# Storing the second layer's edge coefficients in the first pass over the edges of a graph kernel

## The chip, the core and the metric

The kernel runs on one core of a Trainium2 chip. The metric is the device time of one execution in microseconds (us). Three executions of the kernel before gave 28895.52, 28902.54 and 28908.87 us; the median is 28902.54 us. A separate execution was recorded by the hardware profiler; it took 34449.25 us, and its span from the first to the last instruction is 34447.5 us. The two figures are kept apart throughout: durations come from the profiled execution, the comparison of kernels from the others.

The engines are TensorE (PE; its weight loads stand as PEld), VectorE (DVE), ScalarE (ACT), GpSimd (POOL) and SyncE (SP). SP, ACT and POOL also issue DMA transfers. SBUF is the memory of the engines, PSUM the one into which PE writes.

## The reference

There are N = 30000 nodes with 128 features each and E = 960000 edges, sorted by destination. Two residual graph layers follow one another; each begins with a layer norm and a ReLU of the node features. The first is made of two relational convolutions with the same edges:

```python
W   = einsum('rb,bdf->rdf', coeff, basis)     # 32 relations from 8 bases
Hr  = einsum('nd,rdf->nrf', h, W)
msg = Hr[src, etype] * norm                   # norm: one weight for each edge
agg = segment_sum(msg, dst, num_segments=N) + bias
```

The first convolution uses `basis1` and `coeff1` and ends in a ReLU, the second `basis2` and `coeff2`. The second layer is gated: with four edge types t, it sums sigmoid(k[dst] + q[src]) * v[src] over the edges of each type and averages the types.

For an edge of relation r with weight w, the kernel needs only the 8 numbers w * coeff[r, 0..7]. These are the edge's coefficients. The relation and the weight are the same in both convolutions; the coefficient table is not.

## The kernel before, in words

**Three passes over the edges.** After a preparation (layer norm, tables of edge offsets) the kernel makes three passes, called c1, c2 and g: the two convolutions, then the gate. An edge tile is 128 edges; three tiles are a group, five groups a block, twenty blocks (100 groups, 300 tiles) an iteration, and each pass is a hardware loop of 25 iterations with the twenty blocks written out (lines 312 to 327). So a pass has 7500 tiles and 500 blocks.

**One tile of c1 or c2.** GpSimd fetches the 128 source rows of 512 bytes with an indirect DMA into `hg` (line 435). VectorE builds `sb`, 128 edges by 8 bases by 32 destinations, in one instruction: where the edge's offset `relc` equals the column number held in `iw`, it puts the edge's coefficient `ce`, elsewhere zero (line 439). TensorE multiplies the two and sums the three tiles of a group in the PSUM tile `pa` (line 445). ScalarE copies `pa` to `ab` (line 449). Once per block TensorE multiplies `ab` by the eight bases into `po` (line 407, 8 multiplications, each of which stands as two records in the profile[...]). VectorE adds `po` to the running sums `agg` of all nodes, window by window, two blocks later (line 359).

**The coefficients of a block** (lines 376 to 402). SyncE loads the relations of the block's edges as `er`, each repeated on 32 partitions, 256 KB (`types`, line 378). VectorE compares them with the partition number into the one-hot `oh` (`onehot`, line 385). TensorE multiplies four 128-column parts of `oh` by the coefficient table (line 390; 32 columns: 4 edge quarters by 8 bases) into `pc`, which is a part of the PSUM tile `cp`. VectorE multiplies `pc` by the edge weights `nrm` into `ce` (`coefficients`, line 399). Both passes do all of this.

**The order of the work.** It is written out by hand; each engine works through its queue in that order. In block s, `types(s + 2)` is issued at the start; `bases_out(s - 1)` follows group 1, `coefficients(s + 1)` group 2, `onehot(s + 2)` and the additions of block s - 2 group 3. At the start of an iteration stand `loads(0)`, `types(0)`, `onehot(0)`, `coefficients(0)`, `types(1)`, `onehot(1)`, ahead of the first `sb` (lines 412 to 417); at its end stand the last `bases_out` and the additions of the last two blocks (lines 461 to 463). `cp` also holds `iw`, which every `sb` reads.

**Buffers.** `hg` has five buffers of one group each: the gathers of group n + 5 wait until TensorE has used group n. `sb` has twelve buffers of one tile, `pa` three, `er`, `oh` and `ce` two. Beside the edges, each pass carries node work in its queues (line 460, `beside`): `after_first` in c1, `after_second` in c2, every ninth group.

Of the kernel before, what the change touches and what calls it, by code (L numbers as in the profile page):

```python
# [9 lines left out]
F32 = mybir.dt.float32  # L10
# [8 lines left out]
P = 128  # L19
# [7 lines left out]
R = 32  # L27
B = 8
T = 4
TP = 128  # L30
NT = E // TP
G = 3
# [37 lines left out]
def kernel(  # L70
# [39 lines left out]
    kcode = nc.dram_tensor("kcode", (E,), F32, kind="Internal").ap()  # L110
    qidx = nc.dram_tensor("qidx", (TP, NT), I32, kind="Internal").ap()

    def gather(to, table, idx):
# [28 lines left out]

    basis, coeff = [], []
    for i, (bas, cof) in enumerate(((basis1, coeff1), (basis2, coeff2))):
        ct = consts.tile([P, 4, B], F32, name=f"coeff{i}")
        nc.vector.memset(ct, 0.0)
        for q in range(4):
            nc.scalar.dma_start(ct[q * R:(q + 1) * R, q, :], cof)
        basis.append(bas)
        coeff.append(ct)  # L150

# [142 lines left out]
    def sorted_path():  # L294
        with ExitStack() as all_:
            def edge_pass(name, body, after, banks, extra=None):


                with ExitStack() as held:
                    weights = held.enter_context(tc.tile_pool(name=f"{name}_w", bufs=1))  # L300
                    steps, run = after(weights), body(weights)
                    with tc.tile_pool(name=f"{name}_io", bufs=NQ) as io, \
                            tc.tile_pool(name=f"{name}", bufs=2) as pool, \
                            tc.tile_pool(name=f"{name}_n", bufs=1) as npool, \
                            tc.tile_pool(name=f"{name}_nps", bufs=banks, space=PSUM) as nps, \
                            tc.tile_pool(name=f"{name}_c", bufs=1, space=PSUM) as cps, \
                            tc.tile_pool(name=f"{name}_ps", bufs=2, space=PSUM) as ps:
                        cp = cps.tile([P, 4 * D], F32, name="cp")
                        iw, ic = cp[:, :W], cp[:, W:W + 1]
                        nc.vector.tensor_copy(iw, irow)  # L310
                        nc.vector.tensor_copy(ic, icol)
                        with tc.For_i(0, NI, 1, iteration_sync="staggered") as i:
                            with tc.manual_schedule():
                                todo = {}
                                for n, step_ in extra(i, npool) if extra else ():
                                    todo.setdefault(n, []).append(step_)
                                for u in range(NPI // VB):
                                    at = i * -NPI + (N + LAG + u * VB)
                                    for n, step in steps(at, npool, nps):
                                        todo.setdefault(u * PERIOD + n, []).append(step)  # L320
                                assert W < TQ * 4 * B and max(todo) < NG

                                def beside(n):
                                    for step in todo.get(n, ()):
                                        step()

                                run(i, io, pool, ps, cp, iw, ic, beside)
# [32 lines left out]

            def rel_body(table, weights, cof):
                def start(npool):
# [4 lines left out]
                def body(bas, i, io, pool, ps, cp, iw, ic, beside):  # L367
                    stage = {}
                    er, oh, pc, ce, ab, po, base = {}, {}, {}, {}, {}, {}, {}

                    def loads(k):
                        stage[k] = [stage_tile(io, "idx", src, I32, i, k),
                                    stage_tile(io, "relc", reld, F32, i, k),
                                    stage_tile(io, "nrm", norm, F32, i, k, 4 * TQ - S * G)]

# [7 lines left out]
                    def onehot(s):  # L383
                        oh[s] = pool.tile([P, TQ, TP], F32, name="oh")
                        nc.vector.tensor_scalar(oh[s], er[s], icol4, None, op0=ALU.is_equal)
                        at = (1 + s % 2) * TQ * 4 * B
                        pc[s] = cp[:TP, at:at + TQ * 4 * B].rearrange("p (c q b) -> p c q b",
                                                                      c=TQ, q=4)
                        for c in range(TQ):
                            nc.tensor.matmul(pc[s][:, c].rearrange("p q b -> p (q b)"),  # L390
                                             lhsT=oh[s][:, c, :],
                                             rhs=cof.rearrange("p q b -> p (q b)"),
                                             start=True, stop=True)

                    def coefficients(s):
                        ce[s] = pool.tile([TP, 4, TQ, B], F32, name="ce")
                        t0 = s % SB * S * G
                        nrm = stage[s // SB][2][:, t0:t0 + 4 * TQ]
                        nc.vector.tensor_mul(
                            ce[s], pc[s].rearrange("p c q b -> p q c b"),  # L400
                            nrm.rearrange("p (q c) -> p q c", q=4).unsqueeze(3).to_broadcast(
                                [TP, 4, TQ, B]))

# [8 lines left out]
                    loads(0)  # L412
                    types(0)
                    onehot(0)
                    coefficients(0)
                    types(1)
                    onehot(1)
                    for s in range(NS):
# [6 lines left out]
                        if s % SB == 2:  # L425
                            leave_stage()
                        idx, relc, _ = stage[k]
                        if s + 2 < NS:
                            types(s + 2)
                        ab[s] = pool.tile([P, B, S, W], F32, name="ab")  # L430
                        for g in range(S):
# [5 lines left out]
                            for j in range(G):  # L437
# [3 lines left out]
                                    relc[:, t0 + j:t0 + j + 1],  # L441
                                    ce[s].rearrange("p q c b -> p (q c) b")[
                                        :, g * G + j, :].unsqueeze(2).to_broadcast([TP, B, W]),
                                    op0=ALU.is_equal, op1=ALU.mult)
# [5 lines left out]
                            if g == 1 and s:  # L450
                                bases_out(s - 1)
                            if g == 2 and s + 1 < NS:
                                coefficients(s + 1)
                            if g == 3 and s + 2 < NS:
                                onehot(s + 2)
                            if g == 3 and s > 1:
# [269 lines left out]

            edge_pass("c1", rel_body(h0, basis[0], coeff[0]), after_first, 2, codes)
            edge_pass("c2", rel_body(h1, basis[1], coeff[1]), after_second, 2)
            edge_pass("g", lambda weights: gate_body, after_third, 1)


    def any_path():
        with ExitStack() as all_:
# [60 lines left out]
            def rel_conv(table, to, weights, cof, relu):  # L794
                bas = cs.tile([P, B, D], F32, name="bas", bufs=2)
                nc.scalar.dma_start(bas, weights.rearrange("b d f -> d b f"))
                with tc.tile_pool(name="slow", bufs=2) as pool, \
# [18 lines left out]
                    for j in range(G):  # L816
                        nc.tensor.matmul(pc[:, j, :], lhsT=oh[:, j, :], rhs=cof[:R, 0], start=True,
                                         stop=True)
# [23 lines left out]

            rel_conv(h0, agg1, basis[0], coeff[0], False)
            rel_conv(agg1, agg2, basis[1], coeff[1], True)

# [116 lines left out]
```

## Time and profile before

| | before |
|---|---|
| median of three executions | 28902.54 us |
| profiled execution | 34449.25 us |
| its span | 34447.5 us |
| POOL busy in the span | 21410.1 us (62%) |
| PE busy | 20497.2 us (60%) |
| DVE busy | 12592.8 us (37%) |
| ACT busy | 3659.3 us (11%) |
| first to last gather of c1 | 192.6 to 11386.4 us |
| of c2 | 11431.9 to 22747.1 us |
| of g | 22865.2 to 34419.0 us |

A line of a group of instructions names the source line, the engine, the operation and the tiles (written first, then read), the number of instructions, the busy time and the mean of one, and then the idle time of the engine just before them with what ended most of it. "issue" means that nothing which the profile shows was waited for. "remote" stands where a semaphore was raised at a moment that fits the end of no recorded instruction. In a timeline the two figures ahead of the engine are the start and the length in us, and the bracket gives the idle time before and what ended it; several instructions of a kind in a row share one line.

### The profile page before, as it was taken

Reading aid. Unit: us, or ns where it says so; the run is one execution under the profiler, and the core shown is the slowest. Engines: PE = TensorE matmul, PEld = TensorE weight load, DVE = VectorE, ACT = ScalarE, POOL = GpSimd, SP = SyncE. Lnnn points to the kernel's source line nnn. Section 1 sums busy time; section 2 is a strip of 40 time slices with the busy share of each in tenths; the row PEclk is TensorE's granted clock in tenths of the full one; section 3 lists DMA queues with packets and bytes.
Section 4 is the critical chain, followed back from the end, with each engine's and each line's share of the span. In section 5 each row is a group of like instructions: output and inputs, shape, how many; then the busy total and the mean of one; then the engine's idle time right before and its main releaser. Section 6 shows DMA issues by size and latency. Waiting matters only on the chain. (4 is left out here: it accounts for less than half of the span.)

```text
span 34447.5 us, 320361 instructions
## 1 busy us (share of the span) xinstructions
PE 20497.2 (60%) x87408; PEld 17662.1 (51%) x87408; DVE 12592.8 (37%) x33274; ACT 3659.3 (11%) x9905; POOL 21410.1 (62%) x22514
## 2 busy tenths in 40 slices
PE   4555555555555566666666666665555555555555
PEld 3444544444444445545555454445555555555555
DVE  3333333333333333333333333333333333333333
ACT  1000000000000111111111111111111111111111
POOL 5666666666666566666666666656666666666666
PEclk7777777777777777777777777765555555555555
DMA  3222222222222222222222222234444444444444
GB/s 97 62 62 62 63 61 62 63 63 62 62 62 62 70 73 73 73 74 72 72 73 73 73 73 73 73 107 145 145 144 144 144 144 146 145 144 144 146 143 141
DMA packets 2182999, 3244.35 MB, mean 94 GB/s; under 512 B 551918, under 2 KB 1559594, under 8 KB 2181290
## 3 DMA queue, kind: packets, MB, share of 16 engines
q0 software_dynamic: 840000, 1967.52, 20.6%
q1 hardware_dynamic: 993620, 1001.65, 9.0%
q10 hardware_dynamic: 347670, 254.20, 2.6%
q8 instruction: 852, 13.96, 0.2%
q14 instruction: 857, 7.02, 0.1%
HBM read 2969.29 MB, written 252.28 MB: 94 GB/s over the span
## 5 line engine op out<-in xcount | busy, mean ns | idle before, releaser
L114 POOL DMA_INDIRECT hg<-h,idx x15000 | 14273.0, 952 | 8446.5 <-issue 4105.1
L445 PE MATMUL pa<-sb,hg 128*128 128x256 f32 x30000 | 9304.2, 468 | 5934.2 <-issue 2892.9
L445 PEld LDWEIGHTS pa<-sb,hg 128*128 128x128 f32 x30000 | 6919.2, 240 | 7715.2 <-issue 3346.1
L114 POOL DMA_INDIRECT qv<-qvtab,qi x7500 | 7109.3, 948 | 4562.6 <-issue 2220.3
L439 DVE SCALAR_TENSOR_TENSOR sb<-cp,relc,ce 128x256 f32<-128x256 f32 x15000 | 6134.1, 476 | 6576.0 <-remote 4679.9
L510 PE MATMUL po<-sel,msg 128*128 128x32 f32 x15000 | 3471.0, 388 | 4592.1 <-DVE msg L508 3824.5
L510 PEld LDWEIGHTS po<-sel,msg 128*128 128x128 f32 x15000 | 3420.4, 328 | 4894.5 <-DVE msg L508 3986.6
L499 PE MATMUL pk<-kw,kb 128*128 128x128 f32 x15000 | 3973.5, 438 | 219.5 <-DVE kb L486 178.4
L540 DVE TENSOR_TENSOR pk<-pk,qv 128x384 f32<-128x384 f32 x2500 | 1406.8, 563 | 7074.9 <-remote 4837.9
L449 ACT COPY ab<-pa 128x256 f32<-128x256 f32 x5000 | 1816.6, 373 | 20148.8 <-remote 8809.6
L499 PEld LDWEIGHTS pk<-kw,kb 128*128 128x128 f32 x15000 | 3466.7, 331 | 222.3 <-issue 222.3
L407 PE MATMUL po<-ab,bas 128*128 128x160 f32 x16000 | 2431.3, 306 | 311.2 <-ACT ab L449 262.8
L407 PEld LDWEIGHTS po<-ab,bas 128*128 128x128 f32 x16000 | 2356.8, 196 | 408.4 <-ACT ab L449 291.0
L359 DVE TENSOR_TENSOR agg<-agg,po 128x32 f32 x7500 | 1402.9, 187 | 2742.5 <-remote 709.7
L541 ACT ACTIVATE pk<-pk 128x384 f32<-128x384 f32 x2500 | 1186.7, 475 | 9493.7 <-DVE pk L540 6531.3
L390 PE MATMUL cp<-coeff,oh 128*128 128x32 f32 x8000 | 1313.4, 297 | 1472.0 <-issue 1173.2
L390 PEld LDWEIGHTS cp<-coeff,oh 128*128 128x128 f32 x8000 | 1394.2, 237 | 1530.9 <-issue 1308.1
L637 PE MATMUL bank<-wall,hT 128*120 128x512 f32 x1572 | 1012.0, 765 | 710.2 <-issue 307.3
L508 DVE TENSOR_TENSOR msg<-pk,qv 128x384 f32<-128x384 f32 x2500 | 1368.0, 548 | 19.4 <-remote 19.4
L486 DVE TENSOR_TENSOR kb<-kb,cp 128x1920 f32<-128x1920 f32 x500 | 1072.7, 2145 | 52.0 <-issue 29.6
L637 PEld LDWEIGHTS bank<-wall,hT 128*120 128x120 f32 x1572 | 345.9, 235 | 988.0 <-issue 581.2
L648 DVE TENSOR_TENSOR kt<-bank,ball 120x512 f32<-120x512 f32 x262 | 181.2, 692 | 1484.0 <-remote 509.2
(77 smaller groups left out, 3762.9 us busy)
## 6 DMA issues: line engine op xcount, KB each, us to landing
kb<-kcode SPq DMA_DIRECT2D x500, 960.0 KB
er<-in_et_row SPq DMA_DIRECT2D x1000, 256.0 KB
hg<-h,idx POOLq DMA_INDIRECT x15000
kw<-ktab SPq DMA_DIRECT2D x2500, 64.0 KB
qvtab<-qvt ACTq DMA_DIRECT2D x262, 480.0 KB
qv<-qvtab,qi POOLq DMA_INDIRECT x7500
ktab<-kt ACTq DMA_DIRECT2D x262, 240.0 KB
xt<-in_x SPq DMA_DIRECT2D x262, 60.0 KB
```

Of the source, the lines that this page charges most:

```text
L114: nc.gpsimd.indirect_dma_start(out=to, out_offset=None, in_=table, in_offset=bass.IndirectOffsetOnAxis(ap=idx, axis=0))
L359: nc.vector.tensor_add(to, to, po[:, g, :])
L390: nc.tensor.matmul(pc[s][:, c].rearrange("p q b -> p (q b)"), lhsT=oh[s][:, c, :], rhs=cof.rearrange("p q b -> p (q b)"), start=True, stop ...
L407: nc.tensor.matmul(po[s].rearrange("p s w -> p (s w)"), lhsT=bas[:, b, :], rhs=ab[s][:, b].rearrange("p s w -> p (s w)"), start=(b == 0), ...
L439: nc.vector.scalar_tensor_tensor(sb, iw[:TP].unsqueeze(1).to_broadcast([TP, B, W]), relc[:, t0 + j:t0 + j + 1], ce[s].rearrange("p q c b - ...
L445: nc.tensor.matmul(pa.rearrange("p b w -> p (b w)"), lhsT=hg[:, j, :], rhs=sb.rearrange("p b w -> p (b w)"), start=(j == 0), stop=(j == G ...
L449: nc.scalar.copy(ab[s][:, :, g, :], pa)
L499: nc.tensor.matmul(pk[n][:, j, :], lhsT=kb[n // S][:, n % S, j * TP:(j + 1) * TP], rhs=kw[n], start=True, stop=True)
L508: nc.vector.tensor_mul(msg, pk[n], qv[n][:, :, 1, :])
L510: nc.tensor.matmul(po[s][:, g, :], lhsT=msg[:, j, :], rhs=sel[s][:, g * G + j, :], start=(j == 0), stop=(j == G - 1))
L540: nc.vector.tensor_add(pk[n], pk[n], qv[n][:, :, 0, :])
L637: nc.tensor.matmul(bank(a, VB, T * D), lhsT=hT, rhs=wall[:, a].rearrange("p t f -> p (t f)"), start=True, stop=True)
```

## The change

The first pass forms the coefficients of both convolutions, since edges and weights are the same. The coefficient table becomes one tile with both layers side by side, so that a one-hot multiplication gives 64 columns instead of 32. Two multiplications by the edge weights follow, one for each layer. The second layer's result is stored by ScalarE's queue into a new DRAM tensor `ce2`, 128 rows of 480 bytes for each block. The second pass has no `er`, no `nrm`, no `onehot` and no `coefficients`; SyncE loads the block's coefficients from `ce2` two blocks ahead, into four buffers. `pc` now takes 256 columns of `cp` and has one place instead of two.

```diff
+    ce2 = nc.dram_tensor("ce2", (NI * NS, TP, S * G * B), F32, kind="Internal").ap()
...
-        ct = consts.tile([P, 4, B], F32, name=f"coeff{i}")
+    coeff = consts.tile([P, 4, 2, B], F32, name="coeff")
...
                     def loads(k):
                         stage[k] = [stage_tile(io, "idx", src, I32, i, k),
-                                    stage_tile(io, "relc", reld, F32, i, k),
-                                    stage_tile(io, "nrm", norm, F32, i, k, 4 * TQ - S * G)]
+                                    stage_tile(io, "relc", reld, F32, i, k)]
+                        if not second:
+                            stage[k].append(
+                                stage_tile(io, "nrm", norm, F32, i, k, 4 * TQ - S * G))
...
-                        at = (1 + s % 2) * TQ * 4 * B
-                        pc[s] = cp[:TP, at:at + TQ * 4 * B].rearrange("p (c q b) -> p c q b",
-                                                                      c=TQ, q=4)
+                        at = TQ * 8 * B
+                        pc[s] = cp[:TP, at:2 * at].rearrange("p (c q l b) -> p c q l b", c=TQ, q=4,
+                                                             l=2)
                         for c in range(TQ):
-                            nc.tensor.matmul(pc[s][:, c].rearrange("p q b -> p (q b)"),
+                            nc.tensor.matmul(pc[s][:, c].rearrange("p q l b -> p (q l b)"),
                                              lhsT=oh[s][:, c, :],
-                                             rhs=cof.rearrange("p q b -> p (q b)"),
+                                             rhs=coeff.rearrange("p q l b -> p (q l b)"),
                                              start=True, stop=True)
...
                     def coefficients(s):
-                        ce[s] = pool.tile([TP, 4, TQ, B], F32, name="ce")
...
+                        for to, l in ((ce, 0), (ce_next, 1)):
+                            to[s] = pool.tile([TP, 4, TQ, B], F32, name=f"ce{l}")
+                            nc.vector.tensor_mul(
+                                to[s], pc[s][:, :, :, l].rearrange("p c q b -> p q c b"),
+                                nrm.rearrange("p (q c) -> p q c", q=4).unsqueeze(3).to_broadcast(
+                                    [TP, 4, TQ, B]))
+                            to[s] = to[s].rearrange("p q c b -> p (q c) b")
+
+                    def block_rows(s):
+                        return ce2[ds(i * NS + s, 1)].rearrange("o p e -> (o p) e")
+
+                    def keep(s):
+                        nc.scalar.dma_start(block_rows(s), ce_next[s][:, :S * G, :].rearrange(
+                            "p t b -> p (t b)"))
+
+                    def kept(s):
+                        ce[s] = pool.tile([TP, S * G, B], F32, name="ce", bufs=4)
+                        nc.sync.dma_start(ce[s].rearrange("p t b -> p (t b)"), block_rows(s))
...
                     loads(0)
-                    types(0)
-                    onehot(0)
-                    coefficients(0)
-                    types(1)
-                    onehot(1)
+                    if second:
+                        kept(0)
+                        kept(1)
+                    else:
+                        types(0)
+                        onehot(0)
+                        coefficients(0)
+                        types(1)
+                        onehot(1)
...
                         if s + 2 < NS:
-                            types(s + 2)
+                            (kept if second else types)(s + 2)
...
-                            if g == 2 and s + 1 < NS:
+                            if g == 2 and not second and s + 1 < NS:
                                 coefficients(s + 1)
-                            if g == 3 and s + 2 < NS:
-                                onehot(s + 2)
+                            if g == 3 and not second:
+                                keep(s)
+                                if s + 2 < NS:
+                                    onehot(s + 2)
...
-            edge_pass("c1", rel_body(h0, basis[0], coeff[0]), after_first, 2, codes)
-            edge_pass("c2", rel_body(h1, basis[1], coeff[1]), after_second, 2)
+            edge_pass("c1", rel_body(h0, basis[0], False), after_first, 2, codes)
+            edge_pass("c2", rel_body(h1, basis[1], True), after_second, 2)
```

A second path of the kernel, for edges that are not sorted, is touched only in how it reads the coefficient table; it does not run here.

## The prediction

> **What bounds the kernel now.** I read the chain of waits first. It covers only the last iteration's tail (all its shares are 0%), so it names no bound. The engine totals come next:
>
> ```profile
> PE 20497.2 (60%) x87408; PEld 17662.1 (51%) x87408; DVE 12592.8 (37%) x33274; ACT 3659.3 (11%) x9905; POOL 21410.1 (62%) x22514
> L114 POOL DMA_INDIRECT hg<-h,idx x15000 | 14273.0, 952 | 8446.5 <-issue 4105.1
> ```
>
> No engine is full. GpSimd (POOL) leads, and nearly all of it is 22500 gathers. I then cut the span at the first and last gather of each pass (passes c1, c2, g):
>
> ```profile
> 192.00:11387.00 11195.00, 6444.45 (x27479) 5491.36 (x27480) 3842.64 (x11315) 1008.21 (x2997) 7154.69 (x7500) 0.74 0.23 62
> 11432.00:22748.00 11316.00, 7205.69 (x29480) 5674.99 (x29480) 4393.45 (x12740) 1182.26 (x3497) 7117.82 (x7500) 0.78 0.26 73
> 22865.00:34420.00 11555.00, 6755.83 (x30225) 6451.16 (x30226) 4208.52 (x8486) 1330.40 (x3024) 7109.30 (x7500) 0.51 0.47 144
> ```
>
> The columns are the stretch, its length, the busy time of PE, PEld, DVE, ACT and POOL, the PE clock, the DMA share and GB/s. In c2, PE works 7.2 of 11.3 ms and DVE 4.4. Three quite different passes take nearly the same time, which their common 7500 gathers explain.
>
> From the starts of successive gathers I take the pitch: the median is 1.2525 us (0.95 of work, 0.30 between). The ledger of the profiled execution: 22497 pitches inside passes x 1.2525 = 28177.5; 192.6 before the first gather, 45.4 and 118.2 between passes, 28.5 after the last, together 384.7; the three passes last 34062.8, so 5885 is waiting beyond the pitch. Sum 34447.5; with 1.75 around the span it is the profiled 34449.25.
>
> The median of the plain runs is 28902.54, 5547 less. If pitch and ends are the same there, 28902.5 - 1.75 - 384.7 - 28177.5 = 339 us of waiting is left, against 5885. I therefore take GpSimd's pitch as what sets the plain run, and most waits of the profile as the recording's own. In them several engines stop together and resume within a microsecond, and PE's semaphore rises in a dense row long after the recorded ends of its matmuls ("remote").
>
> What is left to win or lose must act on GpSimd. Two places do. The first is the start of an iteration, here of c2:
>
> ```profile
> 12332.85 0.95 POOL L114 DMA_INDIRECT hg<-h,idx  x1 [0.30 <-issue]
> ...
> 12347.18 1.08 DVE L359 TENSOR_TENSOR agg<-agg,po 128x32 f32 x5 [6.47 <-PE po L407]
> 12349.42 0.55 DVE L385 TENSOR_SCALAR oh<-er,icol 128x512 f32<-128x512 int32 x1 [1.15 <-issue]
> 12350.11 1.05 PE L390 MATMUL cp<-coeff,oh 128*128 128x32 f32 x8 [3.67 <-issue]
> 12357.32 0.29 DVE L399 TENSOR_TENSOR ce<-cp,nrm 128x128 f32<-128x128 f32 x1 [7.35 <-remote]
> 12358.06 1.91 PE L390 MATMUL cp<-coeff,oh 128*128 128x32 f32 x8 [6.90 <-DVE oh L385]
> 12360.01 3.62 DVE L439 SCALAR_TENSOR_TENSOR sb<-cp,relc,ce 128x256 f32<-128x256 f32 x9 [2.01 <-PE cp L390]
> 12363.75 0.95 POOL L114 DMA_INDIRECT hg<-h,idx  x1 [9.03 <-PE pa L445]
> 12364.91 0.48 DVE L385 TENSOR_SCALAR oh<-er,icol 128x512 f32<-128x512 int32 x1
> 12365.00 1.21 POOL L114 DMA_INDIRECT hg<-h,idx  x1 [0.30 <-issue]
> ```
>
> The new iteration's gathers start at 12332.85. GpSimd can run 15 ahead, then waits for group 0 to be used. Group 0 waits for DVE to end the old iteration, then for the opening: one-hot, PE, `ce`, one-hot, PE, and only then `sb` (it reads `iw` in the tile that line 390 writes). Over 24 such starts the wait at the sixth group averages 8.96 us in c2, 5.78 in c1, 8.09 in g; the first eight groups wait 12.4, 9.4 and 11 us.
>
> The second place is the last pair: a gather beside an `oh` takes 1.21 instead of 0.95 us. Of the 500 `oh` of c2, 140 have such a gather next to them, 166 ns longer on average, 313 at most, 23 us in all. `sb` and `ce` lengthen none to speak of.
>
> [...] `oh` lengthens gathers, `ce` doesn't. [...] `ce2` has rows of 480 B; the trace of before has 551918 packets under 512 B, none of them this store.
>
> **The change part by part.**
>
> *c2 loses the opening and the coefficients.* Per block:
>
> ```profile
> L385 DVE TENSOR_SCALAR oh<-er,icol 128x512 f32<-128x512 int32 x500 | 245.5, 491 | 39.7 <-issue 28.0 <-DMA er<-in_et_row 11.7
> L399 DVE TENSOR_TENSOR ce<-cp,nrm 128x128 f32<-128x128 f32 x500 | 141.0, 282 | 151.1 <-remote 140.7 <-PE cp L390 8.3 <-issue 2.1
> L390 PE MATMUL cp<-coeff,oh 128*128 128x32 f32 x4000 | 658.1, 299 | 724.1 <-issue 494.3 <-DVE oh L385 206.8 <-remote 13.7
> ```
>
> 386 us of DVE and 658 us of PE go; both engines wait for gathers most of the time, so this counts nothing by itself. If the gathers were no cover, it would be worth up to those sums.
>
> What reaches GpSimd: (a) the port. 23 us in the profiled execution. In a steady plain run `oh` falls at a fixed phase of the gathers, so it may hit none or all: 0 to 500 x 0.313 = 157 us. I take -30. (b) The start of the iteration. Without the recording's delays, I rebuild the chain from the rows: last gather lands 2 to 3.6 us after its issue, `pa` 0.7, copy 0.5, `bases_out` 2.4 to 4.6, additions 1.1, loop 1.2, opening 5 to 6, `sb` and PE of group 0 about 1.5: 13 to 18 us after the new start, against 15 x 1.2525 = 18.8 us of cover. So the wait is near its threshold: 0 at the low end. At the high end, of the 339 us left I take off the long gathers (62 in c1, 25 in c2) and give the rest, 252, to the 72 starts by the profile's shares: 3.5 each, 4.0 in c2, 24 x 4.0 = 95 us. I take -40. Removing the opening moves `sb` about 5 us earlier, more than 4.0.
>
> *Loads.* SP issues 500 `ce` loads (60 KB) in place of 500 `er` (256 KB) and 100 `nrm`. SP was already well into the next iteration before DVE ended the old one, and four buffers let `ce` come two blocks (37 us) early; hidden by that lead. Were it gone, the start would wait a load's landing, some 2 us x 24 = 48. Lower DMA load: DMA is busy a quarter, so 0.
>
> *c1 gains.* PE: line 390 with 64 columns. Lower bound 0 (the eight records are 0.11 to 0.22 us apart, no closer to their columns than to their weight loads); upper 0.1 x 8 per block = 400 us of PE, covered by PE's 4.7 ms of idle time there. DVE: a second multiply, 500 x 0.28 = 141 us, covered likewise, and no port. `pc` has one place now: its PE write waits for the multiplies, which precede the `oh` in DVE's queue anyway, so no new wait. ACT: 500 stores. An `h` store takes 0.335 us to issue plus about 0.1 of address work: 500 x 0.44 = 220 us on an engine busy 1.0 of 11.2 ms; behind it stands the copy of group 4's `pa`, of which three buffers and the five of `hg` are the cover. `ce_next` has two buffers: DVE overwrites one a block after its store was issued (18.8 us; an `out_x` store landed in 2.3). At an iteration's start c1's opening grows by 0.2 (multiply ahead of the second `oh`) to 1.0 us (with PE), 24 times: 0 to +24. I take +8.
>
> Sum: -30 - 40 + 8 = -62. The profiled execution, on its own terms, loses more: 23 plus most of 24 x 8.96 = 215, so about 34449 - 200 = 34250[...]. For the plain run: 28902.5 - 62 = 28840.
>
> **The rivals.**
>
> *Main (0.54): GpSimd's pitch sets the time, and port and starts give a little.* 28840; own range 28902.5 - 157 - 95 = 28650 to 28902.5 + 24 = 28927.
>
> *A: all hidden (0.26).* [...] the starts are covered. For it: the rebuilt chain mostly stays under 18.8. Against: 252 us of waiting that nothing else explains. 28895.
>
> *B: the profile's waits are in the plain run too (0.12),* with a pitch shorter than 1.25 there. Then most of c2's 24 x 12.4 = 298 us goes: 28600. Against: the ledger closes so well with 1.2525.
>
> *C: slower (0.08).* The stores hold ACT in c1. If each waited on its predecessor's landing[...], `pa` copies come late, PE stops, and `hg` is not freed. It decides only where a hold exceeds the ring's slack, 18.8 less landing and use, over 10 us a block; each 0.2 us beyond costs 500 x 0.2 = 100: 29000. Against: landings near 2 us.
>
> That the change does not do what it says is excluded: c2's instructions aren't issued at all.
>
> **How the numbers follow.** 0.2% is 58 us, about what a measurement tells from no change. Main lies across it: 0.36 beyond, 0.18 within. Faster 0.36 + 0.12 = 0.48; same 0.18 + 0.26 = 0.44; slower 0.08. The range 28650 to 28940 holds main and A and leaves out B's lower part and C.
>
> **What would show it.** In the profile after: no lines for `er`, `oh` and the multiply in c2; the wait at the sixth group of c2's iterations down from 8.96 to under 4 us, with `sb` directly behind the additions; no gathers of 1.1 us or more in c2; the pitch unchanged at 1.25; c1's as before, its start up to 1 us longer. Wrong would make me: a pitch that moves, c1 longer by over 50 us, or a c2 start that waits for `ce` loads.

## The result and the profile after

The changed kernel takes 28821.47 us (median of 10 runs, 28812.31 to 28834.99), the kernel before, run beside it, 28903.4 us (10 runs, 28882.95 to 28912.14). The ratio is 0.9973, with a 95 % interval of 0.9963 to 0.9982; by the medians the change saves 82 us, or 0.28 %. The prediction said 28840.

The chips were not alike: on one of them every kernel took 34.1 to 34.5 ms in all its runs, as the recording did that the prediction was read from; elsewhere the times were 28.7 to 29.0 ms. So two recordings of the kernel before are used here, the one shown with the prediction and a later one (`e0_before_again`) of 28.9 ms.

The engine totals and the gathers of the page of the changed kernel:

```profile
PE 21110.4 (73%) x83408; PEld 16304.6 (57%) x83408; DVE 12440.2 (43%) x32773; ACT 3730.9 (13%) x9905; POOL 21302.0 (74%) x22514
L115 POOL DMA_INDIRECT hg<-h,idx x15000 | 14185.2, 946 | 4828.1 <-issue 3963.0
L386 DVE TENSOR_SCALAR oh<-er,icol 128x512 f32<-128x512 int32 x500 | 249.0, 498 | 47.8 <-issue 31.9 <-DMA er<-in_et_row 15.9
L401 DVE TENSOR_TENSOR ce<-cp,nrm 128x128 f32<-128x128 f32 x1000 | 239.9, 282 | 50.7 <-PE cp L391 50.7
L391 PE MATMUL cp<-coeff,oh 128*128 128x64 f32 x4000 | 626.3, 311 | 249.4 <-DVE oh L386 249.4
```

Half of the comparisons are gone (500 `oh`, all in c1), the multiplications are still 1000 (two per block of c1), and the 4000 records of the coefficient product are one pass's, with 64 columns: 311 ns each, against 306 with 32 columns in the later recording of the kernel before. GpSimd still leads, now with 74 %.

The same cut by passes as in the prediction, at the first and last gather, after the change:

```profile
197.00:9632.00 9435.00, 6925.84 (x27480) 5132.69 (x27480) 3963.46 (x11820) 1055.37 (x2999) 7108.73 (x7500) 0.83 0.30 77
9679.00:19042.00 9363.00, 7251.72 (x25480) 4671.73 (x25480) 4067.42 (x11745) 1214.01 (x3499) 7076.43 (x7500) 0.85 0.30 77
19162.00:28791.00 9629.00, 6834.31 (x30232) 6452.16 (x30232) 4263.24 (x8486) 1324.15 (x3024) 7089.15 (x7500) 0.51 0.58 173
```

and in the later recording of the kernel before:

```profile
193.00:9620.00 9427.00, 7017.49 (x27479) 5217.33 (x27479) 3859.52 (x11320) 1045.32 (x2999) 7105.52 (x7500) 0.82 0.28 74
9667.00:19077.00 9410.00, 7311.37 (x29479) 5463.95 (x29480) 4384.55 (x12745) 1212.39 (x3499) 7100.03 (x7500) 0.84 0.33 88
19197.00:28850.00 9653.00, 6883.60 (x30226) 6478.48 (x30226) 4262.73 (x8486) 1322.29 (x3024) 7088.07 (x7500) 0.51 0.57 173
```

The columns are those of the prediction. DVE's busy time in c2 falls from 4385 to 4067 us and the number of its instructions by 1000, but what counts is the length of the pass. From first to last gather: c1 9426.7 before, 9432.9 after; c2 9409.3 and 9361.5; g 9653.1 and 9627.1. With the stretches around the passes (+4.7, +0.9, +1.5, and -1.9 at the end) the two spans differ by 4.7 + 6.2 + 0.9 - 47.8 + 1.5 - 26.0 - 1.9 = -62.4 us (28878.5 and 28816.1). The medians differ by 82; the other 20 us stand in no recording.

So c2 gives 48 us and c1 takes 6. The third pass, which the change does not touch, gives 26.

Of c2's 48 us the gathers show two parts. The lines are GpSimd's gathers in c2 (instructions, busy time and mean of one, idle time and what ended it), first of the later recording before, then after:

```profile
L114 POOL DMA_INDIRECT hg<-h,idx x7500 | 7100.8, 947 | 2356.2 <-issue 1814.6 <-PE pa L445 176.6 <-DMA hg<-h,idx 172.3
```

```profile
L115 POOL DMA_INDIRECT hg<-h,idx x7500 | 7076.4, 944 | 2333.6 <-issue 1906.9 <-PE pa L462 165.5 <-PE po L421 116.4
```

Busy falls by 24.4 us: gathers no longer lengthened. Idle falls by 22.6 us. The ordinary gap between gathers is 0.30 us, and whatever ended it is named as its releaser, so most of that idle time is no waiting at all. Real waits are the gaps over 0.345 us, counted from 0.30 on. The kernel before had 24 us of them in c2, 20 us of it ended by the landing of a gather (the moment at which its data have arrived), mostly at groups 31, 40, 41 and 49 of the iteration. The kernel after has less than 1 us in all. Its 25 iterations of c2 follow one another every 374.4 or 374.5 us, once 375.0: 300 gathers at 1.248 us each. **GpSimd now issues without a break throughout c2.**

The start of an iteration of c2 after the change (start, length, engine, line; in brackets the idle time before and its releaser):

```profile
10433.34 0.94 POOL L115 DMA_INDIRECT hg<-h,idx  x1 [0.30 <-issue]
10433.42 1.08 DVE L358 TENSOR_TENSOR agg<-agg,po 128x32 f32 x5 [9.25 <-PE po L421]
10434.58 0.94 POOL L115 DMA_INDIRECT hg<-h,idx  x1 [0.30 <-issue]
10435.63 4.79 DVE L457 SCALAR_TENSOR_TENSOR sb<-cp,relc,ce 128x256 f32<-128x256 f32 x12 [1.13 <-issue]
10435.83 0.94 POOL L115 DMA_INDIRECT hg<-h,idx  x1 [0.30 <-issue]
10436.64 7.13 PE L462 MATMUL pa<-sb,hg 128*128 128x256 f32 x18 [3.26 <-issue]
```

`sb` stands 1.13 us behind the additions, as the prediction said, and no gather waits. But the mean wait at the sixth group of c2's iterations had been under 0.1 us in the later recording before, not 8.96: there was hardly a wait to remove.

### The profile page after: what moved, and what is told of

The parts are those of the page before. It is cut to its first block, busy times and chain, and to the rows that moved or that the text cites. A ratio compares the mean times of both kernels' runs of the same rounds, so it can differ in the third digit from the quotient of the medians.

```text
span 28816.1 us, 313664 instructions
## 1 busy us (share of the span) xinstructions
PE 21110.4 (73%) x83408; PEld 16304.6 (57%) x83408; DVE 12440.2 (43%) x32773; ACT 3730.9 (13%) x9905; POOL 21302.0 (74%) x22514
## 5 line engine op out<-in xcount | busy, mean ns | idle before, releaser
L462 PE MATMUL pa<-sb,hg 128*128 128x256 f32 x30000 | 10207.6, 464 | 4469.8 <-DMA hg<-h,idx 2842.0
L462 PEld LDWEIGHTS pa<-sb,hg 128*128 128x128 f32 x30000 | 5829.2, 221 | 8231.1 <-issue 3993.5
L115 POOL DMA_INDIRECT qv<-qvtab,qi x7500 | 7089.2, 945 | 2659.4 <-issue 2019.8
L421 PEld LDWEIGHTS po<-ab,bas 128*128 128x128 f32 x16000 | 2857.2, 230 | 151.3 <-ACT ab L466 52.3
L421 PE MATMUL po<-ab,bas 128*128 128x160 f32 x16000 | 2873.6, 343 | 23.1 <-ACT ab L466 23.1
L505 DVE TENSOR_TENSOR kb<-kb,cp 128x1920 f32<-128x1920 f32 x500 | 1072.6, 2145 | 47.8 <-issue 29.7
L656 PE MATMUL bank<-wall,hT 128*120 128x512 f32 x1572 | 893.7, 685 | 29.2 <-issue 24.9
L391 PEld LDWEIGHTS cp<-coeff,oh 128*128 128x128 f32 x4000 | 654.9, 234 | 299.7 <-issue 228.5
L391 PE MATMUL cp<-coeff,oh 128*128 128x64 f32 x4000 | 626.3, 311 | 249.4 <-DVE oh L386 249.4
L639 DVE BATCH_NORM_STATS2 st<-bank 120x6 f32<-120x128 f32 x262 | 78.1, 298 | 959.7 <-PE bank L636 959.2
```

The source lines that it names most:

```text
L115: nc.gpsimd.indirect_dma_start(out=to, out_offset=None, in_=table, in_offset=bass.IndirectOffsetOnAxis(ap=idx, axis=0))
L391: nc.tensor.matmul(pc[s][:, c].rearrange("p q l b -> p (q l b)"), lhsT=oh[s][:, c, :], rhs=coeff.rearrange("p q l b -> p (q l b)"), start= ...
L421: nc.tensor.matmul(po[s].rearrange("p s w -> p (s w)"), lhsT=bas[:, b, :], rhs=ab[s][:, b].rearrange("p s w -> p (s w)"), start=(b == 0), ...
L462: nc.tensor.matmul(pa.rearrange("p b w -> p (b w)"), lhsT=hg[:, j, :], rhs=sb.rearrange("p b w -> p (b w)"), start=(j == 0), stop=(j == G ...
```

## The experiments

Three chips carried them. The kernel before took 28936.16 us on the first (29 runs), 34382.89 on the second (36 runs) and 28851.58 on the third (45 runs); each ratio is to the kernel before on the same chip. Times are medians; lengths of passes and lines of gathers come from one recorded execution of each kernel.

**The kernel before, once more** (no edit):

> The kernel before, unchanged, for a second recording of it. If the long waits of its first recording were the recording's own, this span can lie near 28900 us, and then shows where GpSimd waits in c2 of the kernel before. Port theory: in c2 some of the 500 gathers beside a one-hot comparison are longer than 1.0 us, together 30 to 90 us, and the starts of iterations wait under 1 us each. Start theory: 24 starts of c2 wait 2 to 4 us each, 40 to 95 us in all, and long gathers sum to under 25 us. If the waits are real (rival B), the span is again near 34400 us and so are the waits.

This one execution took 28880.23 us, span 28878.5, on the first chip. Here recording did not add 5.5 ms, and the long stops, in which several engines wait together, are not in the trace. Its gathers stand 1.249 us apart in c1 and c2 and 1.251 in g. What exceeds 1.2525 us sums to 65 + 48 + 280 = 393 us in c1, c2 and g, lengthened gathers included; the prediction had deduced 339. In c2 half of the 48 us are lengthened gathers. Of g's 280 us, 254 are still there after the change.

**The port alone.** "Port" is the prediction's word for what lets a comparison on VectorE lengthen a gather. The changed kernel; c2 also compares one constant `er` tile for every block, and nobody reads the result:

```diff
+ nc.vector.tensor_scalar(oh[s], kept_same[0], icol4, None, op0=ALU.is_equal)
```

> The changed kernel, with the one-hot comparison of a block put back into c2 alone, at its old place in VectorE's queue and with nothing hanging on it: 500 more tensor_scalar instructions, and neither the multiplications nor the coefficients of TensorE and VectorE. Port theory: it gives back most of what the change gained, 28870 to 28910 us, with gathers of over 1.0 us in c2. Start theory: no more than 25 us above the changed kernel, about 28830 to 28845. All hidden: 28821.

28881.96 us, ratio 0.998 (0.9972 to 0.9988). GpSimd in c2:

```profile
L115 POOL DMA_INDIRECT hg<-h,idx x7499 | 7100.4, 947 | 2332.5 <-issue 1887.7 <-PE pa L478 156.7 <-PE po L435 103.6
```

Busy returns to the value before (7100.4), idle stays at that after (2332.5). c2 takes 9386.0, 24.5 us more than after the change. That is the whole cost of 500 comparisons that nobody reads: 170 gathers are lengthened, by 24.3 us together.

**The opening alone.** In c2 of the changed kernel each iteration begins as before: the first block's coefficients are formed, and the second block's one-hot is compared and multiplied. The coefficients of the second block, as of all later ones, are loaded:

```diff
- kept(0)
+ types(0)
+ onehot(0)
+ coefficients(0)
+ types(1)
+ onehot(1)
  kept(1)
```

> The changed kernel, with c2's opening of an iteration done as before: the relations of two blocks loaded, compared and multiplied on TensorE, the first block's coefficients formed, then the first sb. From block 1 on the coefficients are read from the store. Start theory: it gives back 40 to 95 us, 28860 to 28915, and the sixth group of c2's iterations waits 2 to 4 us. Port theory: two comparisons in each iteration instead of twenty, so under 10 us, 28821 to 28831, and no wait at the starts.

28869.58 us, ratio 0.9975 (0.9965 to 0.9986). c2 takes 9363.5, 2.0 us over the changed kernel's, and 1.3 us of it are gathers lengthened by the comparisons. The start of an iteration was worth about 2 us on this chip, not 40.

**c1's part alone.** c1 as after the change, c2 as before; the stored coefficients are read by nobody:

```diff
- (kept if second else types)(s + 2)
+ types(s + 2)
```

(and likewise its opening, one-hot, coefficients and weights, with a coefficient table of the second layer's own)

> The first pass as in the changed kernel (64 columns, two multiplications, the store), the second pass forming its own coefficients as before, so the store is read by nobody: the added work without the saved. My sum: 8 us more than before (0 to 24), 28900 to 28930. Rival C: the store holds ScalarE and c1 is longer by 50 us or more, 28960 and up. If the added work were to gain something in c1, it would lie under 28890.

28942.85 us, ratio 1.0001 (0.9993 to 1.0009). The 500 stores, the wider product and the second multiplication cost 7 us, between -20 and +26 by the interval. The stores landed after 1.9 us here, 3.9 in the changed kernel's own recording. (The gathers of this recording stand 1.251 us apart in c1 and c2 instead of 1.249, so its passes are not set beside the others'.)

**The changed kernel on the second chip** (no edit):

> The changed kernel once more, on the same chip as the runs beside it: about 80 us under before, as on record. In its recording c2 takes about 9361 us from its first to its last gather, with under 2 us of waiting.

34170.67 us, ratio 0.9935 (0.9921 to 0.9949), 212 us faster. The lines are GpSimd's gathers in c2, in the recording that the prediction was read from, then here:

```profile
L114 POOL DMA_INDIRECT hg<-h,idx x7500 | 7118.0, 949 | 4242.7 <-issue 1920.0 <-remote 954.3 <-PE pa L445 565.0
```

```profile
L115 POOL DMA_INDIRECT hg<-h,idx x7500 | 7093.8, 946 | 3976.6 <-issue 1942.6 <-remote 1309.7 <-PE pa L462 382.7
```

Busy falls by 24.2 as on the others, but idle by 266. Of GpSimd's waits in the first of the two, the profile puts 293 us down to PE's coefficient product (line 390), which c2 no longer has; the sixth group's wait falls from 8.96 to 1.22 us. That fits the idea that each handover from DVE to PE and back that is taken out of c2 saves time here, but these recordings don't show it: they hold about a quarter of the semaphore rises that the others hold (below), so who ended a wait is uncertain in them. Nor need the two recordings be of the same chip: of c2's 293 us (11315.2 to 11022.6) only the timed 212 are measured side by side.

**The loads alone.** The changed kernel, with c2's `er` loads issued as before and read by nobody:

```diff
+ types(s + 2)
  kept(s + 2)
```

(and one each beside the two at the iteration's start)

> The changed kernel, with the 256 KB load of a block's relations put back into c2 alone, read by nobody; no comparison, no coefficients formed. New theory (landing): in c2 of the kernel before, a tenth of the gathers landed 4.7 us or later after their start, in the changed kernel 3.1 us, and GpSimd's short waits in c2 stand where a load of relations meets the stores of the node tables. Then this kernel's gathers land late again (90% point over 4 us), waits of some 15 to 25 us come back at the groups 31, 40, 41 and 49 of an iteration, and no gather is prolonged. If those waits come from the work on TensorE and VectorE instead, they stay away: c2 within 3 us of the changed kernel. My prediction put the lower DMA load at 0.

34216.64 us, ratio 0.995 (0.9937 to 0.9964): 46 us over the changed kernel on the second chip. Once more on the third chip, where GpSimd has no long stops:

> The changed kernel with the 502 er loads of c2 put back (256 KB each, read by nobody) beside the 500 loads of stored coefficients. Nothing is left out. Theory (the load's traffic delays gathers where it meets the stores of the node tables): on a chip without long stops c2's waits rise from about 1 to 15 to 25 us, at groups 31, 40, 41 and 49, released by the landing of a gather; no lengthened gathers; the landing's 90 % point rises from 3.1 to about 4.6 us; the pass g is as after the change, 9627 us. On a chip with long stops: +30 to +60 us, as in the run before this. Rival (the short waits came of the comparison's or the coefficients' work, not of the load): c2 stays within 5 us of the changed kernel's.

28812.07 us, ratio 0.9986 (0.998 to 0.9993), against 28771.14 for the changed kernel (below): **41 us for loads that nobody reads.** GpSimd in c2:

```profile
L115 POOL DMA_INDIRECT hg<-h,idx x7500 | 7076.1, 943 | 2371.6 <-issue 1772.4 <-DMA hg<-h,idx 313.6 <-PE pa L466 128.0
```

Against the changed kernel's line below, busy is the same and idle is 39 us longer. No gather is lengthened. Of 41 us of real waits, 34 were ended by a gather's landing. The median landing, from the gather's start to the last rise of its semaphore, stays at 2.5 us, but the ninth decile (nine in ten gathers land sooner) is 4.54 instead of 3.11, and 447 of 7500 take over 5 us instead of 8. Mean landings of 5 us and more stand at groups 30, 66, 87 and 88 of the iteration; in the kernel before they stood at 39 and 48. Groups 30, 39, 48 and 66 have the same distance to the node work that comes every ninth group and stores the tables; 87 and 88 have not. I had expected 15 to 25 us and the groups of the kernel before; the time is larger and the places are others, and why is open.

**Another comparison.** The kernel before, with the one-hot as a `tensor_tensor`, both inputs in SBUF:

```diff
- nc.vector.tensor_scalar(oh[s], er[s], icol4, None, op0=ALU.is_equal)
+ nc.vector.tensor_tensor(oh[s], er[s],
+     icol4.unsqueeze(2).to_broadcast([P, TQ, TP]), ALU.is_equal)
```

> The kernel before, with one edit: the one-hot comparison of c1 and c2 is a tensor_tensor with a broadcast column instead of a tensor_scalar. Work, loads and waits stay. Port theory: the prolonged gathers vanish in both passes, 33 us in c1 and 28 us in c2 by their recording, so 40 to 65 us under before, and c2 keeps about 20 us of short waits. If the prolonged gathers come from anything else about that moment (the load's issue, TensorE, ScalarE), they stay, and the time is that of before.

34433.12 us, ratio 1.0014 (1.0008 to 1.0021), slower. One comparison of it in c1, on DVE and on GpSimd:

```profile
3014.28 1.26 DVE L441 SCALAR_TENSOR_TENSOR sb<-cp,relc,ce 128x256 f32<-128x256 f32 x3
3015.45 0.68 DVE L385 TENSOR_TENSOR oh<-er,icol 128x512 f32<-128x512 int32 x1
...
3015.43 1.53 POOL L114 DMA_INDIRECT hg<-h,idx  x1 [0.30 <-issue]
```

The gather takes 1.53 us instead of 0.94. In c1, 286 gathers beside an `oh` are lengthened by over 30 ns, by 422 ns on average; all lengthened gathers of c1 together cost 134 us, against 61 with `tensor_scalar` in the recording that the prediction was read from. That `oh` is a `tensor_scalar` and `ce` a `tensor_tensor` is thus not what divides the harmful from the harmless. My theory for this run fell.

The trace also shows when a gather suffers. In c1, 363 gathers begin while a comparison runs. Where at least 135 ns of the comparison are left at that moment, 323 of 328 are lengthened, each by what is left less 117 to 132 ns (median 127), so by more the longer the comparison still runs; the other five begin in the first 33 ns of the comparison. Where less is left, none is. Of the 226 gathers that are more than 50 ns old when a comparison begins, none is lengthened by over 17 ns; the one shown above is only 20 ns old, and is held. **So a gather that begins second is held, at a point some 127 ns after its start, until the comparison ends.** `tensor_scalar` does the same (109 of 117 in c1 of the changed kernel on the third chip, median 128 ns) and something more: where it begins 340 to 620 ns after a gather's start, 122 of 151 gathers are lengthened, by up to 190 ns, and some comparisons of usually 480 ns take up to 654. With `tensor_tensor` none of 64 gathers is lengthened there.

**Both, with deeper buffers in g.** The changed kernel with the same `tensor_tensor` and eight `qv` buffers in place of five:

> The changed kernel, with two edits that the traces suggest: c1's comparison as tensor_tensor, and eight instead of five buffers for the rows that pass g gathers. By the recording of the changed kernel c1 has 36 us of prolonged gathers and g 254 us of waits for a free buffer. Port theory and buffer theory together: 36 + 200 to 254 us under the changed kernel, 28530 to 28585. If g's waits come from landings later than any ring covers, or from the start of an iteration as such, g keeps over 100 us.

34454.98 us, ratio 1.0017 (1.0009 to 1.0024), slower. c1 takes 11329.7 (99 us of lengthened gathers) and g 11700, now with 13.2 us at the first group of each iteration. It is 284 us above the changed kernel on this chip; c1 is 117 us longer than in that kernel's recording and g 170. The two edits went together, so only the lengthened gathers of c1 are understood; the deeper ring did not help on this chip.

**The column in PSUM.** `sb`, `ce` and the additions read at least one input from PSUM and lengthen no gather: in c2 of the recording that the prediction was read from, no gather that has one of them beside it, and no `oh`, exceeds the median of 0.947 us by more than 15 ns. So the last theory was: only an operation with all inputs in SBUF does. The kernel before, its column of types copied once per pass into a free column of `cp`:

```diff
+ nc.vector.tensor_copy(cp[:, W + 1:W + 2], icol4)
- nc.vector.tensor_scalar(oh[s], er[s], icol4, None, op0=ALU.is_equal)
+ nc.vector.tensor_tensor(oh[s], er[s],
+     cp[:, W + 1:W + 2].unsqueeze(2).to_broadcast([P, TQ, TP]), ALU.is_equal)
```

> The kernel before, with the one-hot comparison of both passes written as a tensor_tensor whose second input, the column of types, stands in PSUM (a free column of cp); er stays in SBUF. Nothing is left out. Theory (a DVE operation lengthens a gather only where all its inputs are in SBUF): no gather is lengthened beside oh in either pass, though those beside the codes operations of c1 stay; lengthened gathers fall from about 25 us to under 2 in c2, and from 36 to 62 us to under 20 in c1; the short waits at groups 31, 40, 41 and 49 of c2 stay, about 20 us (on a chip with long stops they can't be told apart). Ratio to the kernel before about 0.998, -40 to -65 us. Rival (the length of the operation counts, 128x512 elements, whatever it reads): lengthened gathers stay, 60 us or more in c2 as with two SBUF inputs, and the ratio is 1.001 or above.

28816.69 us, ratio 0.9987 (0.9981 to 0.9994), 35 us faster than before. The same place as above:

```profile
4183.36 0.68 DVE L387 TENSOR_TENSOR oh<-er,cp 128x512 f32<-128x512 int32 x1
...
4183.57 0.95 POOL L114 DMA_INDIRECT hg<-h,idx  x1 [0.30 <-issue]
```

The comparison is as long as with two inputs in SBUF (0.68 us), and the gather that begins beside it takes 0.95. In c1, 183 gathers begin with at least 135 ns of a comparison left, and none of them is lengthened; of all 626 gathers beside an `oh` in c1 none is by over 9 ns, of 675 in c2 none by over 17. For this comparison the memory that the second input comes from decides, not the operation and not its length. (The run with both inputs in SBUF was on another chip; the `tensor_scalar` beside it in the numbers above was on this one.)

c2 of this kernel isolates the rest:

```profile
L114 POOL DMA_INDIRECT hg<-h,idx x7499 | 7075.3, 943 | 2362.4 <-issue 1737.0 <-DMA hg<-h,idx 313.3 <-PE pa L450 134.7
```

With the coefficients still formed but no lengthened gather, idle is 30 us over the changed kernel's: the cost of the loads and the work together, no more than that of the loads alone (39). So the loads alone are enough for these waits.

**The changed kernel with the column in PSUM**, and **the changed kernel** as reference on the same chip (no edit):

> The changed kernel with its only one-hot comparison, c1's, reading its column from PSUM in the same way. Nothing is left out. Theory: it loses c1's lengthened gathers as well, 20 to 40 us below the changed kernel, a ratio to the kernel before of about 0.996 (0.9925 on a chip with long stops). Against it: the second comparison of an iteration's start now stands behind the matmuls that write the same tile, 1 to 2 us at 24 starts, which would take up to 40 us back if those starts were not covered; the changed kernel without long stops had about 0.1 us of waiting there, so I expect under 5 us. Rival (length counts): no gain on the changed kernel, or a loss of up to 100 us.

> The changed kernel, as reference on the same chip for the two above. Ratio to the kernel before 0.996 to 0.999 on a chip without long stops, about 0.9935 on one with them.

28745.23 us, ratio 0.9966 (0.9951 to 0.998), and 28771.14 us, ratio 0.9973 (0.9963 to 0.9983). The version with the column in PSUM is 26 us below the changed kernel, and their runs do not overlap (28731.89 to 28758.9 and 28764.27 to 28781.2): the fastest of all. But c1, where the edit is, took 9420.8 us in both recordings. GpSimd in c1, with the column in PSUM, then the changed kernel, and third the changed kernel's c2, for the comparisons above:

```profile
L115 POOL DMA_INDIRECT hg<-h,idx x7500 | 7084.3, 945 | 2501.6 <-issue 1953.4 <-DMA hg<-h,idx 316.9 <-PE pa L467 120.1
```

```profile
L115 POOL DMA_INDIRECT hg<-h,idx x7500 | 7106.5, 948 | 2479.7 <-issue 1956.1 <-DMA hg<-h,idx 291.1 <-PE pa L462 113.3
...
L115 POOL DMA_INDIRECT hg<-h,idx x7500 | 7076.2, 943 | 2332.6 <-issue 1784.1 <-DMA hg<-h,idx 285.3 <-PE pa L462 96.6
```

Busy falls by 22.2 us and idle rises by 21.9. Of the real waits, those ended by a landing rise from 23 to 36 us: c1 still has its `er` loads, and the freed gathers come sooner to such a wait. Those ended by PE rise from 3 to 12 us; the sixth group of an iteration now waits 0.47 us instead of 0.14, as the second comparison reads the tile that PE writes. So c1 explains none of the timed 26 us. In the recordings (28756.35 and 28769.84 us) g is 17 us shorter, which nothing in the edit explains; the source of the gain is not shown.

## Why the prediction was right, and where it was wrong

**The bound held.** "GpSimd's pitch sets the time": c2 now consists of nothing but 7500 gathers at 1.248 us, and the 386 us of DVE and 658 us of PE taken out of it were worth nothing by themselves. Its gain is the lengthened gathers and the late landings. The pitch did not move with the change (1.249 us before and after in c1 and c2). It is below the 1.2525 that the ledger used: with 1.249 in c1 and c2 and 1.251 in g, the same sum leaves 28902.5 - 1.75 - 384.7 - 28113.8 = 402 us of waits instead of 339.

**The port, -30: right.** c2's busy line fell by 24.4 us, and the comparison put back alone costs 24.5. The pair that the prediction set side by side, `oh` and `ce`, could not show what divides them: `ce` differs from `oh` not only in its operation but reads one input from PSUM. The run with both inputs in SBUF (286 gathers of c1 lengthened) and the one with a PSUM column (none of 626 by over 9 ns) tell the two apart: with the same operation and the same 0.68 us, the place of the second input decides. A gather that begins second, with at least 135 ns of the comparison left, is held until it ends (323 of 328; 582 ns at most, for a comparison of 682), and one that begins more than 50 ns earlier is not held by a `tensor_tensor`. The runs show when and by how much; why is not shown.

**The start of an iteration, -40: wrong in size.** The step put 252 us of waits that nothing else explained at the 72 starts, "by the profile's shares". Those shares came from the recording with the long stops. The waits are there, but in the later recording 280 of 393 us stand in g, and only a third of these at its starts (3.7 us at each; 3.1 after the change). c2's sixth group had waited under 0.1 us, and the opening put back alone costs 2.0 us. The rebuilt chain of 13 to 18 us against 18.8 of cover, a few lines earlier, had it right: covered.

**Lower DMA load, 0: wrong.** "DMA is busy a quarter, so 0" took the mean share for the answer. The five buffers of `hg` are a ring that lets a gather land late by only so much, and where the 256 KB loads ran beside them 447 of 7500 gathers took over 5 us to land, against 8 without, and 34 us of GpSimd's waits were ended by a landing; whether a load has to meet a table's store for it stays open. In the kernel before that was worth some 20 us of c2's idle line; the loads alone cost 41 us timed, 39 in the line. This term made up for the missing start.

**c1, +8: right**, +6.2 in the recordings, and c1's part alone +7 timed. The stores did not hold ACT (0.338 us to issue one, 0.367 at most), so rival C fell.

**"The recording's own": rightly left out, but its cause is open.** The plain runs did not have the 5885 us, and on the first and third chip recordings don't have them either. On the second chip all executions take over 34 ms, not only the one whose trace was kept; but each of them lists a granted clock and a span, as a recorded execution does, so what that chip takes with nothing recorded is not known. And its recordings are not whole: the five of about 34.4 ms hold 148445 to 156097 semaphore rises, the nine of about 28.8 ms 544519 to 554965. Of the 33795 rises that VectorE's instructions of the kernel before announce, the first recording holds 17936, the later one 33770. So the loss of records and the stops go together, and whether the recording stops the engines there, as the prediction assumed, or something else causes both, no run tells. It also means that "PE's semaphore rises" long after its matmuls, on which the prediction leaned, stand in a record with gaps. The figure that step produced for "its own terms", a loss of about 200 us, was met by the timed 212, and rival B, most of c2's start waits gone, fits the times of that chip. Rival A, all hidden, fell with the two parts of c2.

**The third pass, -26: not foreseen.** In the recordings g idles longer where c2 forms its coefficients (2684.0, 2683.7 and 2673.6 us) than where it does not, or only in part (2659.4, 2649.3, 2659.0, 2616.8, 2616.5 and 2629.6). The loads alone and the comparison alone are both on the low side, so neither causes it alone. The difference is spread over the iterations; some 15 us of it lie at the sixth group (3.7 us at each start before, 3.1 after). What causes it stays open. The chips differ as well: on the third the low side is lower.

The sum of -62 agrees with the recordings' -62 by luck: -40 and 0 should have been about -2 and -20, and the 26 us of g were in no term.

## What to carry to other kernels

Where one engine issues at a fixed pitch, look for what lengthens its instructions and what makes its buffers come back late; busy time removed elsewhere was worth nothing here. Moving one input of a comparison to PSUM freed the gathers beside it (none of 626 in c1 lengthened by over 9 ns), but what a freed gather gains can go into a wait behind it: the edit came with 35 us in the kernel before, and with nothing in c1 of the changed kernel, where 22.2 us less of busy time met 21.9 us more of idle time. Before a recording's waits are read as the kernel's or blamed on the recorder, look whether the record is whole, and time the kernel on the same chip with nothing recorded.

## What the runs showed that I had not expected

- A gather that began while a `tensor_tensor` comparison of 128x512 elements with both inputs in SBUF ran, and at least 135 ns of it were left, was held until it ended (323 of 328, by 582 ns at most); one that began more than 50 ns earlier was not (226, none by over 17 ns). With one input in PSUM, the comparison of the same 0.68 us held none of 183.
- 256 KB loads moved the ninth decile of a gather's landing from 3.11 to 4.54 us while the DMA engines were busy 28 and 32 % of c2.
- The same kernel took 28936, 34383 and 28852 us on the first, second and third chip. On the second GpSimd's gathers kept their pitch (1.249 to 1.252 us in c1 and c2), and the difference was waiting.
- 64 columns cost PE 311 ns a record where 32 columns cost 306.
